# When transfers are issued around a decoder's last cross attention: gated weights, kept tokens, and the first two weight blocks of the MLP

## The chip, the cores and the metric

The kernel runs on one core of a Trainium2 chip. The time is device microseconds (us) of one execution. The kernel before takes 1160.57 us, the median of three runs (1159.35 to 1161.3). Engines are named as in the profile: PE is TensorE, DVE is VectorE, ACT is ScalarE, POOL is GpSimd, SP is SyncE, which here issues almost all DMAs.

## The reference

Sixteen sequences x of 128 tokens and 512 features go through a decoder layer and then through a gated cross attention. Both attend to sequences of the same shape, ctx_2048. All is float32, with 16 heads of 32 features. In short:

```python
# decoder layer
ln = layernorm(x);   q, k, v = split(ln @ w_qkv + b_qkv)
x = x + merge(attention(q, k, v, ltor_mask)) @ w_ao + b_ao          # sections A0..A3
ln = layernorm(x);   q = ln @ w_q + b_q
k, v = split(ctx_2048 @ w_kv + b_kv)
x = x + merge(attention(q, k, v, cross_mask)) @ w_co + b_co         # sections B0..B3
ln = layernorm(x);   x = x + gelu(ln @ w1 + b1) @ w2 + b2           # w1: 512x2048, w2: 2048x512
# gated cross attention
a = layernorm(ctx_2048)
Q, K, V = x @ Wq.T, a @ Wk.T, a @ Wv.T
x = x + tanh(gate) * (merge(softmax(mask(Q K^T * scale)) V) @ Wo.T) # sections D0..D3
```

## The kernel before, in words

**Sections and steps.** The sixteen sequences are cut into four groups of four. The decoder's attention runs as eight sections, self attention A0 to A3 and then cross attention B0 to B3, one for each group. A section has 16 steps (`attend`, line 685): a step works on one unit, that is four of the sixteen heads of one sequence. In the first of a sequence's four steps PE makes the scores of all heads. The units then go down a chain, one step behind the other: DVE scales the scores, POOL adds the mask, DVE takes the least, ACT takes the exponential, POOL divides by the sums, and DVE transposes 32x32 squares (`turn_unit`, line 598). SP sends the result to DRAM (`away_B<-s_B`, 256 KB a unit). Some steps later it fetches two units at a time, in four transfers of 128 KB (`receive_pair`, line 621, `pT_B<-away_B`), so that the probabilities lie turned. PE mixes the values with them (`av_B`) and two steps later makes the output product (`mo_B`). The pT tiles have three buffers. In the last section, steps go on past 15 until all is mixed.

**Beside a section** other work is placed by hand, by step: `jobs()` of section n+1 (its projections) and `prepare(p)` of section n+2 run in section n's steps. `plan(...)` takes pairs of a list of jobs and a list of their steps. What stands behind B3 is `first`, a `FirstGated`: its `prepare` runs beside B2, and `beside_last_cross()` (line 1721) gives the jobs beside B3: the first gated section's keys and values (`mm_k_D`, `mm_v_D`, whose weights are `w_gk` and `w_gv`), the beginning of the MLP, and the return of x3.

**x3, put away and back.** Each cross section's group of tokens x[g] lends three of its four blocks as room for sums (`tokens_at` in `CrossAttention.jobs`). These blocks are first put away in DRAM (`kept_x_B`) and come back by `tokens_again(steps, order)` (line 1065), before the output products add to them. For B0 to B2 they come back in steps 5, 9 and 13 of the next section, for B3 in steps 1, 1 and 3 of its own.

**Gated weights.** Turned once, early in the kernel, and kept in DRAM as `kept_gk` and `kept_gv`. `FirstGated.prepare` loads each in four pieces of 256 KB, one a step: gk in steps 8 to 11 beside B2, gv in steps 12 to 15. All large weights share a pool of six buffers (tag "w").

**The MLP** (`mlp`, a generator) has 16 rounds n, four groups by four blocks i of 512 hidden features. A round has seven places r, and in each a product of the hidden layer (`h`) and one of the output of the round before (`o`). Products are by quarters with seven products in place of eight, so each weight block needs four sums of its quarters (`weight_sums`, tile t, 1 MB). For the first group these sums are made and put away in DRAM for the other three: `kept<-t`. For round 0 that is done at fixed places, (0, 3) and (1, 3). For later rounds it is a fifth entry of the list `todo` that `sums` returns (line 1222). In round n the sums of w2's block n and of w1's block n+1 stand in one queue, `todo`, and two entries are done at each r. Round 0 begins in step 17 of B3.

`w1_0` is loaded in four pieces beside B2 (steps 12 to 15). Then `pieces` holds four pieces each of `w2_0` and `w1_1`, and `loads` gives the steps beside B3 in which they are issued. `w2_1` and `w1_2`, 1 MB each, are loaded whole in round 0 at r = 1 and r = 2.

**What sets the order.** Every instruction is kept in program order on its engine (`InOrder`). SP takes its DMAs strictly one after the other: one that waits for data holds all behind it. Each also waits until the transfer issued eight places before it has landed. `due()` runs what was put off with `afterwards("act" or "dve", ...)`, at the next step or the next place of the MLP.

Of the kernel before, what the change touches and what calls it, by code (L numbers as in the profile page):

```python
# [10 lines left out]
F32 = mybir.dt.float32  # L11
# [5 lines left out]
P = 128  # L17
# [4 lines left out]
H = 512  # L22
NH = 16
HD = 32
KC = H // P
HALF = H // 2
GB = 4
# [27 lines left out]
def decoder_then_gated_cross_attention(ctx: ExitStack, tc: tile.TileContext, a: dict, out: bass.AP):  # L55
    nc = InOrder(tc)

    cpool = ctx.enter_context(tc.tile_pool(name="const", bufs=1))
    wpool = ctx.enter_context(tc.tile_pool(name="weights", bufs=6))
# [98 lines left out]
    w = {}  # L158
# [843 lines left out]
    class CrossAttention(Section):  # L1002
# [34 lines left out]
        def jobs(self):  # L1037
            g, n, lnT, encT = self.g, self.name, self.lnT, self.encT
            mask = work.tile([P, 2, GB, S], F32, tag="mask", name=f"mask_{g}", bufs=2)
            self.ms, self.ma = mask[:, 0], mask[:, 1]  # L1040
            nc.sync.dma_start(
                out=self.ms, in_=a["mask_Bx1xSxS2_ff1"][g * GB : (g + 1) * GB, 0].rearrange("b q k -> q b k")
            )
            qkv_tiles(self)
            tokens_at = [x[g][:, b].rearrange("p (o t) -> p o t", t=HF) for b in range(3)]
            token_sides, sums = right_blocks(encT, tokens_at)
            if g == 0:
                self.begin()
            products = [
                block_product(halves(self.k), self.k_sides, token_sides, False, f"k_{n}", ("b_k", 0)),  # L1050
                block_product(by_quarters(self.v), self.v_sides, token_sides, True, f"v_{n}"),
            ]
            return plan(
                ([lambda c=c: self.query_chunk(c) for c in range(KC)], [0, 1, 3, 5]),
                *blocks_plan(products, CROSS_BLOCKS if g else FIRST_CROSS_BLOCKS), ([lambda: mask_terms(self.ms, self.ma)], [7]),
                ([lambda o=o: nc.gpsimd.tensor_tensor(*o) for o in sums], [0, 1, 2, 3]),
                *(self.weights_begin() if g == 0 else decoder[NG + g - 1].tokens_again([5, 9, 13])),
            )

        def query_chunk(self, c):  # L1060
# [117 lines left out]
    def mlp(ml, last_steps):  # L1178
# [17 lines left out]
        def load(n, which):  # L1196
            g, i = steps[n]
            ap, r0, c0 = (a["L0_xattn_w1"], 0, i * H) if which == 1 else (a["L0_xattn_w2"], i * H, 0)
            wt = wpool.tile([P, KC, H], F32, tag="w", name=f"w{which}_{n}")
            src = ap[r0 : r0 + H, c0 : c0 + H].rearrange("(k p) n -> p k n", p=P)  # L1200
            if n < 2 and not (n == 1 and which == 2):
                for k in range(KC):
                    pieces.append(lambda k=k: nc.sync.dma_start(out=wt[:, k], in_=src[:, k]))
            elif g == 0:
                nc.sync.dma_start(out=wt, in_=src)
            else:
                nc.sync.dma_start(out=wt[:, 0:2, 0:HF], in_=src[:, 0:2, 0:HF])
                nc.sync.dma_start(out=wt[:, 2:4, :], in_=src[:, 2:4, :])
            return wt
# [114 lines left out]

        w1[0] = load(0, 1)
        yield
        w2[0], w1[1] = load(0, 2), load(1, 1)
        right1[0], todo, _ = sums(0, 1, "enc", w1.pop(0), nc.gpsimd)
        yield
        for do in todo:  # L1330
# [7 lines left out]
        for n in range(len(steps) + 1):  # L1338
            todo, more = deque(), []
            at_ = {r: [] for r in range(7)}  # L1340
            h = lnT = None
            if n + 1 < len(steps):
                right1[n + 1], more, back = sums(n + 1, 1, "v", w1.pop(n + 1))
                at_[3].append(back)
            if n < len(steps):
                g, i = steps[n]
                right2[n], first, back = sums(n, 2, "enc", w2.pop(n))
                todo.extend(first + more)
                at_[4].append(back)
                h = work.tile([P, KC, TG], F32, tag="qT", name=f"h_{n}", bufs=2)  # L1350
                if i == 0 and n:
                    sides = following
                if g + 1 < NG and i == 1:
                    at_[0].append(lambda: ml_begin(g + 1))
                    for b in range(GB):
                        at_[b].append(lambda b=b: ml_send(g + 1, b))
                elif g + 1 < NG and i == 2:
                    lnT = turned_tile(g + 1)
                    at_[0].append(lambda: ml_receive(g + 1))
                    for m in range(NQ):  # L1360
                        at_[m // 2].append(lambda m=m: ml.part(m))
                    for c in range(KC):
                        at_[3 + c].append(
                            lambda c=c: chunk_back(lnT[c // 2][:, c % 2], ml.back, c, "ln3_s", "ln3_b")
                        )
                    next_lnT = lnT
                elif g + 1 < NG and i == 3:
                    following, more = sums_of(g + 1, next_lnT)
                    for r, do in enumerate(more):
                        at_[3 + r].append(do)  # L1370
            if before is not None:
                for r, do in enumerate(before[1]):
                    at_[r].append(do)
            for r in range(7):
                if n < len(steps):
                    p = H_ORDER[r]
                    hidden_product(n, p, sides[p], right1[n][p], h)
                if before is not None:
                    p = O_ORDER[r]
                    out_product(n - 1, p, before[0][p], right2[n - 1][p], acc)  # L1380
                for _ in range(min(2, len(todo))):
                    todo.popleft()()
                for do in at_[r]:
                    if do is not None:
                        do()
                if r == 1 and n + 1 < len(steps):
                    w2[n + 1] = load(n + 1, 2)
                elif r == 2 and n + 2 < len(steps):
                    w1[n + 2] = load(n + 2, 1)
                last_steps(n, r)  # L1390
                if (n, r) in ((0, 3), (1, 3)):
                    d, t = unkept.pop(0)
                    nc.sync.dma_start(out=d, in_=t)
                yield
            if n < len(steps):
                t = work.tile([P, 3, 2, HF], F32, tag="kT", name=f"sh_{n}", bufs=2)
                before = token_sums(halves(h), t[:, 0], t[:, 1], t[:, 2])


    gated = {}  # L1400
# [56 lines left out]

    class FirstGated:


        def prepare(self, p):
            if p == 0:
                self.raw = work.tile([P, GB, H], F32, tag="enc", name="enc_D0", bufs=2)
                self.ln, self.away = ln_tile("D0"), away_tile("D0")
            if p in (0, 1):
                for b in (2 * p, 2 * p + 1):
                    nc.sync.dma_start(out=self.raw[:, b, :], in_=a["ctx_2048"][b])
            elif p >= 2 * GB:
                key, k = ("gk", "gv")[p // GB - 2], p % GB
                if k == 0:  # L1470
                    w[key] = wpool.tile([P, KC, H], F32, tag="w", name=f"w_{key}")
                nc.sync.dma_start(out=w[key][:, k], in_=gated[key][:, k])
            if 2 <= p < 6:
                q = p - 2
                normalize_and_send(self.raw[:, q, :], self.ln[:, q], self.away, "D0", q)
            if p >= 12:
                if p == 12:
                    next(in_mlp)
                ml.pieces.popleft()()
            if p in (9, 11):  # L1480
                if p == 9:
                    self.back, self.part = receiver("a0", self.away)
                for m in range(2):
                    self.part(m + 2 * (p == 11))
            if p >= 12:
                if p == 12:
                    self.aT = act_tile("a0", "enc")
                group_back(self.aT, self.back, "gamma", "beta", [p - 12])
# [228 lines left out]
    ml = Mlp()  # L1717
# [3 lines left out]
    def beside_last_cross():  # L1721
        flip[0], in_blocks[0] = 2, False
        def piece():
            due()
            next(in_mlp)

        at_ = [2, 3, 4, 5, 6, 15, 15, 16, 16, 17, 18, 19, 19, 20, 21, 21, 22, 23, 23]
        loads = [5, 7, 9, 11, 13, 14, 15, 16]
        return plan(
            *gated_start(first), *mlp_start(ml), *decoder[-1].tokens_again([1, 1, 3], (1, 0, 2)), ([piece] * len(at_), at_),  # L1730
            ([lambda: ml.pieces.popleft()()] * len(loads), loads),
        )

# [94 lines left out]
```

## Time and profile before

| what | us |
| --- | --- |
| median of three runs | 1160.57 |
| the profiled execution, as timed | 1162.35 |
| its span in the profile | 1160.6 |
| PE busy in the span | 1132.9 |
| B2, scores at steps 0, 4, 8, 12 | 403.8, 419.9, 434.9, 451.3 |
| B3, scores at steps 0, 4, 8, 12 | 467.2, 483.2, 496.0, 511.9 |
| first product of the MLP's round 0 (step 17) | 526.5 |

Everything in the profile has the source line L51, since a helper records all operations; so one goes by the names of tiles, and by times. A line of the timeline gives start, duration, engine, what is written and read, and in square brackets how long the engine was idle before it and what released it. In the timeline of SP the durations are those of issuing, not of the transfer. In the chain that ended last, a line "DMA a<-b" gives the time from the issue to the landing.

### The profile page before, as it was taken

Reading aid. Unit: us, or ns where it says so; the run is one execution under the profiler, and the core shown is the slowest. Engines: PE = TensorE matmul, PEld = TensorE weight load, DVE = VectorE, ACT = ScalarE, POOL = GpSimd, SP = SyncE. Lnnn points to the kernel's source line nnn. Section 1 sums busy time; section 2 is a strip of 40 time slices with the busy share of each in tenths; the row PEclk is TensorE's granted clock in tenths of the full one; section 3 lists DMA queues with packets and bytes.
Section 4 is the critical chain, followed back from the end, with each engine's and each line's share of the span. In section 5 each row is a group of like instructions: output and inputs, shape, how many; then the busy total and the mean of one; then the engine's idle time right before and its main releaser. Section 6 shows DMA issues by size and latency. Waiting matters only on the chain.

```text
span 1160.6 us, 22182 instructions
## 1 busy us (share of the span) xinstructions
PE 1132.9 (98%) x7246; PEld 875.1 (75%) x7246; DVE 742.9 (64%) x1919; ACT 612.0 (53%) x2142; POOL 694.4 (60%) x633
## 2 busy tenths in 40 slices
PE   9999999999999999989899999999999999999998
PEld 8877777666666757446688888888888877878875
DVE  6678978798787786866554634443342247767754
ACT  3567676767767766663231233223222237867663
POOL 6798888788868675752333514443342168545883
PEclk9999999999999999989999999999999999999999
DMA  6688878999889889997787696697447827987975
GB/s 220 162 206 227 228 208 212 280 232 255 209 221 222 218 231 254 297 272 247 236 260 238 189 280 192 200 283 254 154 154 234 258 51 200 249 236 222 272 216 175
DMA packets 325285, 259.81 MB, mean 224 GB/s; under 512 B 83561, under 2 KB 280625, under 8 KB 320305
## 3 DMA queue, kind: packets, MB, share of 16 engines
q1 hardware_dynamic: 325128, 258.38, 78.1%
q8 instruction: 58, 0.95, 0.4%
q14 instruction: 59, 0.48, 0.1%
q10 hardware_dynamic: 40, 0.01, 0.0%
HBM read 163.94 MB, written 94.37 MB: 223 GB/s over the span
## 4 chain that ended last, share of the span: by engine, by line
PE 45%; DMA 6%; POOL 2%; DVE 2%; SPq 1%; ACT 1%; issue 1%; DVEq 0%; ACTq 0%; POOLq 0%
PE o L51 16%; PE h L51 15%; PE mm_v_D L51 4%; PE mm_q_D L51 3%; PE mm_o_D L51 1%; DMA back_x<-turned_x 1%; DMA pT_D<-away_D 1%; PE mm_k_D L51 1%; DMA pT_B<-away_B 1%; SPq L51 1%; PE av_D L51 1%; DMA away_D<-s_D 1%; PE mo_D L51 1%; DMA away_B<-s_B 1%; PE sc_D L51 1%
## 5 line engine op out<-in xcount | busy, mean ns | idle before, releaser
L51 DVE TENSOR_TENSOR h<-h,h 128x512 f32<-128x512 f32 x80 | 54.9, 686 | 113.9 <-PE h L51 113.9
L51 ACT ACTIVATE h<-h 128x512 f32<-128x512 f32 x64 | 40.3, 630 | 162.3 <-DVE h L51 162.3
L51 ACT ACTIVATE s_A<-s_A,mn_A 128x128 f32<-128x128 f32 x256 | 99.4, 391 | 45.7 <-issue 23.8
L51 ACT ACTIVATE s_B<-s_B,mn_B 128x128 f32<-128x128 f32 x256 | 99.4, 392 | 29.7 <-issue 14.0
L51 POOL TENSOR_TENSOR s_D<-s_D,sum_D 128x512 f32<-128x512 f32 x64 | 66.5, 1040 | 59.9 <-DVE sum_D L51 53.1
L51 POOL TENSOR_TENSOR s_B<-s_B,sum_B 128x512 f32<-128x512 f32 x64 | 66.8, 1044 | 56.4 <-DVE sum_B L51 47.8
L51 ACT ACTIVATE s_D<-s_D,mn_D 128x128 f32<-128x128 f32 x256 | 99.1, 392 | 0.4 <-issue 0.4
L51 POOL TENSOR_TENSOR s_A<-s_A,sum_A 128x512 f32<-128x512 f32 x64 | 66.5, 1039 | 31.0 <-DVE sum_A L51 25.3
L51 POOL TENSOR_TENSOR s_A<-s_A,ma 128x512 f32<-128x512 f32 x64 | 81.8, 1279 | 5.1 <-DVE s_A L51 4.1
L51 POOL TENSOR_TENSOR s_B<-s_B,mask 128x512 f32<-128x512 f32 x60 | 76.4, 1273 | 2.4 <-DVE s_B L51 1.5
L51 POOL TENSOR_TENSOR rstd_aD<-rstd_aD,mhalf 128x1 f32<-128x1 f32 x12 | 6.6, 549 | 114.8 <-DVE rstd_aD L51 101.6
L51 POOL TENSOR_TENSOR sh<-h 128x512 f32<-128x512 f32 x32 | 40.7, 1272 | 50.8 <-ACT h L51 49.9
L51 PE MATMUL h<-sx,t 128*128 128x256 f32 x256 | 60.6, 379 | 2.0 <-ACT h L51 2.0
L51 PE MATMUL h<-T_C,w 128*128 128x256 f32 x256 | 61.2, 382 | 1.3 <-DVE h L51 1.3
L51 PE MATMUL h<-T_C,t 128*128 128x256 f32 x256 | 60.6, 379 | 1.0 <-DVE h L51 1.0
L51 PE MATMUL o<-t,h 128*128 128x256 f32 x256 | 60.5, 379 | 0.0
L51 PE MATMUL o<-w,h 128*128 128x256 f32 x256 | 60.5, 379 | 0.0
L51 PE MATMUL o<-t,sh 128*128 128x256 f32 x256 | 60.5, 379 | 0.0
L51 DVE CUSTOM_DVE_ANT_0 s_D<-sc_D,gmask 128x128 f32<-128x128 f32 x256 | 57.1, 283 | 1.0 <-DMA turned_x<-x_D 0.9
L51 PE MATMUL mo_A<-w_ao,mT_A 128*128 128x512 f32 x128 | 57.5, 592 | 0.0
L51 PE MATMUL mo_B<-w_co,mT_B 128*128 128x512 f32 x128 | 57.5, 592 | 0.0
L51 PE MATMUL mm_q_B<-T_B,w_cq 128*128 128x512 f32 x128 | 57.4, 596 | 0.0
(335 smaller groups left out, 3007.4 us busy)
## 6 DMA issues: line engine op xcount, KB each, us to landing
t<-kept SPq DMA_DIRECT2D x24, 1024.0 KB, 8.3
away_A<-s_A SPq DMA_DIRECT2D x64, 256.0 KB, 3.3
pT_A<-away_A SPq DMA_DIRECT2D x128, 128.0 KB, 3.8
away_B<-s_B SPq DMA_DIRECT2D x64, 256.0 KB, 3.3
pT_B<-away_B SPq DMA_DIRECT2D x128, 128.0 KB, 4.8
away_D<-s_D SPq DMA_DIRECT2D x60, 256.0 KB, 3.4
pT_D<-away_D SPq DMA_DIRECT2D x120, 128.0 KB, 2.8
w<-in_L_xattn_w_dram SPq DMA_DIRECT2D x24, 512.0 KB, 5.5
```

Of the source, the lines that this page charges most:

```text
L51: return lambda *args, **kw: self.tc.keep_in_program_order(call(*args, **kw))
```

## The change

No operation is added or taken away; on PE, ACT and POOL the instructions and their order are the same. Four places are edited. gk is loaded in steps 14, 14, 15, 15 beside B1, as jobs of B2, and gv in steps 6 to 9 beside B2. x3's blocks come back in steps 6, 10 and 14 of B3, in the order 0, 1, 2. `w1_1` stands ahead of `w2_0` in `pieces`, and the eight pieces are issued in steps 7 to 17. In round 0 alone, `todo` holds w1's entries ahead of w2's. The line numbers of the diff are those of the two files.

```diff
@@ -1055,6 +1055,10 @@  CrossAttention.jobs
                 *(self.weights_begin() if g == 0 else decoder[NG + g - 1].tokens_again([5, 9, 13])),
+                *(
+                    [([lambda k=k: first.fetch_weight_part("gk", k) for k in range(KC)], [14, 14, 15, 15])]
+                    if g == 2 else []
+                ),
             )
@@ -1324,7 +1328,7 @@  mlp
         w1[0] = load(0, 1)
         yield
-        w2[0], w1[1] = load(0, 2), load(1, 1)
+        w1[1], w2[0] = load(1, 1), load(0, 2)
         right1[0], todo, _ = sums(0, 1, "enc", w1.pop(0), nc.gpsimd)
@@ -1345,7 +1349,7 @@  mlp, in round n
                 right2[n], first, back = sums(n, 2, "enc", w2.pop(n))
-                todo.extend(first + more)
+                todo.extend(first + more if n else more + first)
@@ -1457,6 +1461,11 @@
     class FirstGated:
+        def fetch_weight_part(self, key, k):
+            if k == 0:
+                w[key] = wpool.tile([P, KC, H], F32, tag="w", name=f"w_{key}")
+            nc.sync.dma_start(out=w[key][:, k], in_=gated[key][:, k])
+
@@ -1465,11 +1474,8 @@  FirstGated.prepare
-            elif p >= 2 * GB:
-                key, k = ("gk", "gv")[p // GB - 2], p % GB
-                if k == 0:
-                    w[key] = wpool.tile([P, KC, H], F32, tag="w", name=f"w_{key}")
-                nc.sync.dma_start(out=w[key][:, k], in_=gated[key][:, k])
+            elif 6 <= p < 10:
+                self.fetch_weight_part("gv", p - 6)
@@ -1725,9 +1731,9 @@  beside_last_cross
-        loads = [5, 7, 9, 11, 13, 14, 15, 16]
+        loads = [7, 9, 11, 13, 14, 15, 16, 17]
         return plan(
-            *gated_start(first), *mlp_start(ml), *decoder[-1].tokens_again([1, 1, 3], (1, 0, 2)), ([piece] * len(at_), at_),
+            *gated_start(first), *mlp_start(ml), *decoder[-1].tokens_again([6, 10, 14]), ([piece] * len(at_), at_),
```

In the built order of SP's DMAs the last transfers beside B3 change as follows; on DVE the eight sums of `w2_0` and `w1_1` change places.

```
before: w2_1, away_B, w1_2, kept<-t (w1_0), pT_B x4, kept<-t (w1_1)
after:  w2_1, away_B, w1_2, kept<-t (w1_1), kept<-t (w1_0), pT_B x4
```

## The prediction

> **What bounds the kernel now.** I read the busy shares first, then who TensorE (PE) waited for, then PE's timeline at the waits, the DMA share of the same stretches, SyncE's (SP's) issues, and the chain that ended last. The page says that PE is the bound:
>
> ```profile
> PE 1132.9 (98%) x7246; PEld 875.1 (75%) x7246; DVE 742.9 (64%) x1919; ACT 612.0 (53%) x2142; POOL 694.4 (60%) x633
> ```
>
> So the change can only win what PE idles, or add to it: 1160.6 less 1132.9 is 27.7 us in all. PE's waits between 440 and 575 us, where all edits act, name it:
>
> ```profile
> PE av_B L51 <- DMA pT_B<-away_B: 6.7, 2, 5.5
> PE h L51 <- ACT h L51: 2.0, 1, 2.0
> ```
>
> PE's timeline shows where these stand. Square brackets are idle time:
>
> ```profile
> 466.18 1.07 PE L51 MATMUL av_B<-pT_B,v_B 128*32 128x128 f32 x28 [1.12 <-DMA pT_B<-away_B]
> ...
> 510.09 1.92 PE L51 MATMUL av_B<-pT_B,v_B 128*32 128x128 f32 x28 [5.54 <-DMA pT_B<-away_B]
> ...
> 551.57 1.63 PE L51 MATMUL av_B<-pT_B,v_B 128*32 128x128 f32 x32
> 555.16 1.99 PE L51 MATMUL h<-sx,t 128*128 128x256 f32 x8 [1.96 <-ACT h L51]
> ```
>
> I call them stall 1 (466, step 0 of the last cross section, B3), stall 2 (510, B3 step 12) and the tail (552, step 22). At each, probabilities that went out to DRAM come back (pT) too late for a mix (av). The tail's mix is almost late too: its 32 matmuls take 1.63 us against 1.08 us elsewhere. Stall 2 costs more than its 5.54 us, for the clock is halved after it, and the same is seen after a gap of only 2.31 us at 1027 (columns: us, then PE, PEld, DVE, ACT, POOL busy, granted clock, DMA share, GB/s):
>
> ```profile
> 510.00:516.00 6.00, 5.91 (x63) 4.30 (x64) 1.92 (x10) 3.89 (x14) 0.11 (x1) 0.50 1.08 301
> ...
> 1024.60:1028.00 3.40, 1.09 (x32) 0.83 (x28) 3.40 (x15) 0.45 (x3) 2.73 (x3) 1.00 1.02 288
> 1028.00:1031.40 3.40, 3.40 (x11) 2.73 (x9) 0.17 (x2) 0.58 (x1) 2.65 (x3) 0.50 1.09 282
> ```
>
> The same view by stage shows the transfers. A share about 1 means that all 16 DMA engines are busy; then what SP issues waits behind what it issued before:
>
> ```profile
> 446.00:482.00 36.00, 34.88 (x226) 21.96 (x224) 28.97 (x64) 23.02 (x84) 21.25 (x21) 1.00 1.07 294
> 482.00:490.00 8.00, 8.00 (x78) 4.37 (x78) 7.03 (x14) 6.57 (x28) 8.00 (x8) 1.00 0.91 265
> 490.00:512.00 22.00, 16.46 (x128) 8.49 (x126) 14.49 (x29) 12.52 (x58) 17.63 (x16) 0.94 1.08 272
> ```
>
> **Part 1: gk and gv sooner.** Eight 256 KB pieces move, none is added. gk goes from steps 8 to 11 of B2 (436.5 to 447.6) to steps 14 and 15 of B1, where SP issues nothing between 395.7 and 399.3, and the DMA share from 396 to 408 is 0.41: 1 MB at 0.3 MB/us is 3.5 us of room that exists; PE waits for no DMA there. Cost 0. gv goes from steps 12 to 15 of B2 to steps 6 to 9 (428.7 to 438, share 0.69): cost 0. Its first piece gains a wait for PE; the buffer should be that of the query weight, the one that falls free there. The last query product (`mm_q_B`, 423.51, 3.6 us) ends at 427.1; SP gets there at 428.7, behind a `turned_D` send that waits for DVE. If that cover went, the next probabilities' send would be held as long. Two gk and two gv pieces thus vanish from SP's order between 446 and 459.4, ahead of the pT that ends stall 1: 1 MB, at 294 GB/s 3.6 us. The stall is 1.12. **Gain 1.1 us**, and nothing else is late next in that place.
>
> **Part 2: x3 back later.** Three 256 KB pieces leave 469.7, 470.7 and 479.1 for steps 6, 10 and 14 of B3. Their first reader, the addition of `mo_B` after step 14 (DVE at 524.6), comes over 20 us after the step-6 piece, and the third piece's reader is at 543.7. Cost 0 there. Do they relieve stall 2? Only if the queue of 446 to 482 carries over. At 479.7 SP waits 2.4 us for DVE (its next probabilities turned), which it could not if the DMAs were behind, and the share falls to 0.91. So the group that makes stall 2 starts at 482, and in it the change takes out one piece (w2 at step 5) and puts in one (x3 at step 6). Steps 7 and 9 hold w1 instead of w2, same size; the other x3 piece, step 10, is issued behind the late pT. **Stall 2: 0.** Bounds: a piece more or less, 256 KB at 272 GB/s, 0.95 us either way.
>
> **Part 3: w1's second block ahead of w2's first.** The pieces of both are eight before and after, at steps 7 to 17 in place of 5 to 16. DVE's eight sums are the same instructions in another order (0.67 to 1.41 us each); w2's last piece, issued about 532, should land near 536, and DVE reads it at about 536.5: 0, bound +1. But the swapped `todo` also moves an instruction that is not a sum. The list of w1's second block ends with its put-away, a 1 MB transfer to DRAM (`kept<-t`, line 1222). It was the ninth entry, so it stood behind the last pT. It becomes the fifth, and in the built order of SP it stands, with w1's first put-away, **ahead of the last pT**. SP now:
>
> ```profile
> 538.78 0.51 SPq L51 DMA_DIRECT2D w<-in_L_xattn_w_dram  x1
> 539.33 1.08 SPq L51 DMA_DIRECT2D kept<-t  x1
> 544.47 2.13 SPq L51 DMA_DIRECT2D pT_B<-away_B  x4
> 546.70 0.43 SPq L51 DMA_DIRECT2D kept<-t  x1
> ```
>
> What that costs is read from the chain, and from the DVE instruction that waited for the first `kept<-t`:
>
> ```profile
> 538.30 6.09 DMA away_B<-s_B
> ...
> 545.94 6.05 DMA pT_B<-away_B
> ```
>
> ```profile
> 549.64 0.69 DVE L51 TENSOR_TENSOR t<-w 128x512 f32<-128x512 f32 x1 [1.78 <-DMA kept<-t]
> ```
>
> The probabilities' send landed at 544.39, the put-away issued after it at 549.62, with one 1 MB load between: 5.2 us for two such transfers, 2.6 us each. The pT, issued at 544.5 to 546.6, landed at 552.00, behind the put-away. One more put-away in front makes that 554.6. Everything behind is serial: av, ACT's copy of the mix, ACT's h, PE's h at 555.16. DVE's wait for the first put-away grows by as much, and in parallel. **Loss 2.6 us**; bounds 0 (if the pT passes the put-away) and 2.6.
>
> Then the clock. PE's idle time at the tail becomes 0.55 + 2.6 = 3.1 us, followed by 1.08 of work and 1.96 idle. The row at 1024.6 halved the clock for 3.4 us after 2.31 idle, so I expect it here. 3.4 us at half is 1.7 lost, less what falls on the 1.96 us in which PE waits anyway: **loss 1.0**, bounds 0 and 1.7.
>
> [...] The row at 1024.6 gated after 2.31, so I keep the loss. [...] Here the landings kept their order.
>
> **Sum.** −1.1 + 0 + 2.6 + 1.0 = +2.5 us. The profiled execution took 1162.35 us (span 1160.6), 1.8 more than the median of the three runs, 1160.57 (1159.35 to 1161.3). The difference is put on the median: **1163.1 us**.
>
> **The rivals.** What a measurement can tell from no change is about 0.2%, 2.3 us: 1158.2 to 1162.9.
>
> - *Faster: the queue carries over to stall 2.* The share between 482 and 490 is still 0.91, not 0.5. If transfers from before 482 still hold those after it, nine pieces fewer (two gk, four gv, three x3; 2.25 MB, 8 us) bring the pT of step 10 in early. Stall 2 goes with its clock (three groups, 1.92 against 1.08, 2.09 against 1.17, 4.71 against 3.70: 2.8): −1.1 − 5.5 − 2.8 + 3.6 = −5.8, 1154.8. It decides as soon as that pT lands some 3 us earlier, since a short gap spares the clock: 1163.1 − 3 − 2.8 = 1157.3. Against it is SP's wait for DVE at 479.7.
> - *Same: the tail is paid but the clock is not halved, or lightly:* −1.1 + 2.6 = +1.5, 1162.1. [...] Or the last pT is not held: 1159.5.
> - *More slower: stall 2 grows.* The x3 piece at step 6 goes into the group that is late, beside four reads of `turned_C`. A read of kept x took a median 6.2 us to land between 446 and 482, where gv took 4.7. That is 1 us (one piece) to 3 us (two slow reads): 1164.1 to 1166.1.
>
> **How the numbers follow.** Tail with clock, 1163.1: 0.46, of which 0.06 fall under the line at 1162.9. Stall 2 grows: 0.10. Tail without clock: 0.16. Last pT not held: 0.06. Faster, 1154.8 to 1157.3: 0.22. Slower by over 0.2% is 0.40 + 0.10 = 0.50; within, 0.06 + 0.16 + 0.06 = 0.28; faster 0.22. The range takes in half of the faster case, from 1156.5, and most of a grown stall 2 with the full clock loss (+0.7) and w2's late piece (+1), to 1167: about 0.17 is left out. The likeliest case alone is 1162.1 to 1164.8.
>
> **What would show it.** Part 1: no DMA wait of PE near 466, DMA share of 446 to 466 under 1. Part 2: PE's wait near 509 still 5 to 6.5 us, clock 0.50 after it; a wait under 3 us means that the queue carried over, and that I am wrong on the side of faster. Part 3: SP issues two `kept<-t` before the last four pT; PE's wait at the tail's av about 3 us, released by that pT; a granted clock of 0.50 near 556. A wait of DVE for w there means that w2's last piece is late.

## The result, and the profile after

The changed kernel takes 1163.21 us, median of 10 runs (1160.87 to 1166.13). The kernel before, in 10 runs beside it, takes 1159.3 (1157.8 to 1161.3). The ratio is 1.0036, 95% interval 1.0024 to 1.0047: slower by 2.8 to 5.4 us. The profiled execution of the changed kernel took 1166.13 us, with a span of 1164.3, 3.7 more than the span before.

PE is busy for 1.0 us more than before, so the rest of what was lost in this profile is idle time. This line is from the first part of the page:

```profile
PE 1133.9 (97%) x7246; PEld 876.1 (75%) x7246; DVE 742.8 (64%) x1919; ACT 611.9 (53%) x2142; POOL 694.6 (60%) x633
```

PE's waits between 440 and 576 us (total, times, longest) name the same transfer as before, with 9.1 us in place of 6.7:

```profile
PE av_B L51 <- DMA pT_B<-away_B: 9.1, 4, 6.9
PE h L51 <- ACT h L51: 2.0, 1, 2.0
```

PE's timeline of the changed kernel shows where. There is no wait near 466 any more; the other two have grown:

```profile
510.69 1.92 PE L51 MATMUL av_B<-pT_B,v_B 128*32 128x128 f32 x28 [6.95 <-DMA pT_B<-away_B]
...
554.04 1.07 PE L51 MATMUL av_B<-pT_B,v_B 128*32 128x128 f32 x28 [1.74 <-DMA pT_B<-away_B]
557.07 3.78 PE L51 MATMUL h<-sx,t 128*128 128x256 f32 x8 [1.96 <-ACT h L51]
560.64 3.15 PE L51 MATMUL o<-w,h 128*128 128x256 f32 x8
```

The last two lines are at half clock: 3.78 and 3.15 us in place of 1.99 and 1.89. DMA shares by stage in the changed kernel (the last two columns) show less traffic before the group that makes stall 2, and as much in it:

```profile
446.00:482.00 36.00, 36.00 (x257) 22.81 (x257) 28.72 (x64) 22.86 (x84) 21.16 (x22) 1.00 0.87 241
482.00:490.00 8.00, 8.00 (x60) 4.09 (x51) 7.01 (x14) 6.43 (x27) 8.00 (x8) 1.00 0.73 203
490.00:512.00 22.00, 14.78 (x120) 7.64 (x120) 14.64 (x29) 12.66 (x60) 17.79 (x16) 0.92 1.07 284
```

And SP's timeline, between the last send and the last pT, has two put-aways where there was one. The chain that ended last has that pT with 8.47 us from issue to landing in place of 6.05:

```profile
538.71 1.63 SPq L51 DMA_DIRECT2D kept<-t  x2
543.89 2.15 SPq L51 DMA_DIRECT2D pT_B<-away_B  x4
```

```profile
545.43 8.47 DMA pT_B<-away_B
```

The same instructions in the two traces, by their start, give the account. Its first two rows are these lines, before and then after:

```profile
426.95 3.60 PE L51 MATMUL mo_B<-w_co,mT_B 128*128 128x512 f32 x8
467.18 1.17 PE L51 MATMUL sc_B<-k_B,q_B 32*128 32x128 f32 x32
```

```profile
427.45 3.60 PE L51 MATMUL mo_B<-w_co,mT_B 128*128 128x512 f32 x8
466.17 1.17 PE L51 MATMUL sc_B<-k_B,q_B 32*128 32x128 f32 x32
```

"Lead" is after less before; the step is what the stretch above the line added:

| PE instruction | before | after | lead | step |
| --- | --- | --- | --- | --- |
| `mo_B`, 427 (the lead is the same at 351, ahead of all edits) | 426.95 | 427.45 | +0.50 | |
| scores after stall 1 | 467.18 | 466.17 | −1.01 | −1.5 |
| mix after stall 2 | 510.09 | 510.69 | +0.60 | +1.6 |
| `mo_B`, behind the halved clock | 518.51 | 518.50 | 0.0 | −0.6 |
| `h` after the tail's mix | 555.16 | 557.07 | +1.91 | +1.9 |
| `h<-T_C,w`, two products on | 559.38 | 563.63 | +4.25 | +2.3 |
| `h<-T_C,t` | 570.97 | 575.11 | +4.14 | −0.1 |

So stall 1 was won and handed back 40 us later. All that is left at the end was lost at the tail: 1.9 us of waiting, and 2.3 us of half clock behind it. The loss at the tail stands in other profiles too: from the `mo_B` near 518 to `h<-T_C,t` it is 52.46 us before, 56.61 in the changed kernel, and 56.76 in a second profile of it (e5 below). The spans of single profiles are no measure of the change, though: behind `h<-T_C,t`, where no edit acts, the 14 profiles take from 585.4 to 591.7 us, and the span of e5, 1159.6, is below that of before.

### The profile page after: what moved, and what is told of

Read it like the earlier page. It is cut to its first block, busy times and chain, and to the rows that moved or that the text cites. A ratio compares the mean times of both kernels' runs of the same rounds, so it can differ in the third digit from the quotient of the medians.

```text
span 1164.3 us, 22177 instructions
## 1 busy us (share of the span) xinstructions
PE 1133.9 (97%) x7246; PEld 876.1 (75%) x7246; DVE 742.8 (64%) x1919; ACT 611.9 (53%) x2142; POOL 694.6 (60%) x633
## 4 chain that ended last, share of the span: by engine, by line
PE 47%; DMA 4%; POOL 3%; DVE 3%; issue 2%; SPq 1%; ACT 1%; POOLq 0%; DVEq 0%; ACTq 0%
PE o L51 16%; PE h L51 16%; PE mm_v_D L51 4%; PE mm_q_D L51 3%; PE mm_k_D L51 2%; DMA pT_B<-away_B 2%; PE av_D L51 1%; PE mo_B L51 1%; PE sc_D L51 1%; PE mm_o_D L51 1%; POOL s_D L51 1%; DVE s_D L51 1%; SPq L51 1%; POOL x L51 1%; PE mo_D L51 1%
```

## Experiments

The theory after this reading, called A: the loss is the put-away of w1's second block ahead of the last pT, and the clock that its wait brings down; the gain of part 1 is given back at stall 2. Rivals: the tail's wait matters little and stall 2, grown by x3's piece, costs the time (D); or the clock at the tail falls anyway. Each kernel was timed beside the kernel before on the same chip (median of before there: 1160.67 for e1 to e4, 1161.47 for e5 to e8, 1160.74 for e9 to e12). Waits are PE's, in us, in the one profile that each kernel has.

| kernel | ratio to before, 95% | stall 2 | tail's mix | us at half clock after stall 2 / the tail |
| --- | --- | --- | --- | --- |
| before | 1 | 5.54 | 0 | 6.8 / 0 |
| changed | 1.0036, 1.0024 to 1.0047 | 6.95 | 1.74 | 6.8 / 6.8 |
| e1, put-away last | 0.9995, 0.9977 to 1.0014 | 6.82 | 0.42 | 6.8 / 3.4 |
| e2, before with one more put-away | 1.0042, 1.0024 to 1.0061 | 4.44 | 2.52 | 6.8 / 6.8 |
| e3, parts 1 and 2 | 1.0020, 1.0000 to 1.0039 | 6.76 | 1.08 | 10.2 / 3.4 |
| e4, 64 small matmuls at the tail | 1.0040, 1.0023 to 1.0057 | 7.85 | 0 | 6.8 / 0 |
| e5, changed again | 1.0028, 1.0011 to 1.0045 | 6.27 | 2.08 | 6.8 / 6.8 |
| e6, 32 small matmuls | 0.9999, 0.9987 to 1.0011 | 6.53 | 0.59 | 6.8 / 3.4 |
| e7, light group | 1.0006, 0.9991 to 1.0021 | 3.41 | 3.20 | 0 / 6.8 |
| e8, e1 and value products sooner | 0.9987, 0.9971 to 1.0003 | 2.90 | 1.41 | 0 / 3.4 |
| e9, e8 and light group | 0.9977, 0.9958 to 0.9995 | 0.18 | 0 | 0 / 3.4 |
| e10, e9 and 16 small matmuls | 0.9973, 0.9957 to 0.9989 | 0 | 0 | 0 / 0 |
| e11, x3 out of the group | 1.0021, 1.0004 to 1.0039 | 5.06 | 2.05 | 6.8 / 6.8 |
| e12, part 1 alone | 0.9991, 0.9975 to 1.0007 | 5.18 | 0.21 | 6.8 / 3.4 |

### The put-away: e1 takes it away, e2 adds it

e1 is the changed kernel with the put-away behind the sums of w2:

```diff
-                todo.extend(first + more if n else more + first)
+                todo.extend(first + more if n else more[:-1] + first + more[-1:])
```

> The changed kernel, with the 1 MB put-away of w1's second block moved back behind the last four pT transfers; w1's sums still stand ahead of w2's. Theory A (the tail's loss is that put-away ahead of the last pT, and the clock that the longer gap halves): PE's wait at the tail's av falls from 1.74 us to under 0.5, the granted clock stays at 1.00 near 556, and the time falls by 1.6 + 2.3 = 3.9 us, from 1163.2 to about 1159.3; parts 1 and 2 of the change are worth nothing, since stall 2 takes back what stall 1 gives. Rival B (the loss is stall 2 grown by 1.4 us and the order of the sums on DVE): the time stays above 1161.5.

e2 is the kernel before with a second put-away of w1's first block, 1 MB to a spare place in DRAM, issued behind the first one and so ahead of the last pT:

```diff
+                    if n == 0:
+                        spare = dram.tile([P, 4, 2, HF], F32, tag="spare", name="spare")
+                        nc.sync.dma_start(out=spare, in_=t)
```

> The kernel before, with one transfer added and nothing else: w1's first block of sums is put away twice (the second time to spare room), so that one more 1 MB transfer stands ahead of the last four pT. Theory A: the last pT lands about 2.6 us later, PE's wait at the tail's av is 2 to 3 us, and the granted clock is halved near 556; the time rises by 2.6 + 1.0 to 2.6 + 2.3, from 1159.3 to between 1162.5 and 1164.2. Rival B (a transfer there is hidden): 1159.3 to 1160.3.

e1 took 1160.8 us, 0.9995, and e2 1165.64, 1.0042. SP's timeline and PE's in e1:

```profile
538.69 1.41 SPq L51 DMA_DIRECT2D kept<-t  x1
546.42 1.79 SPq L51 DMA_DIRECT2D pT_B<-away_B  x4
548.25 0.43 SPq L51 DMA_DIRECT2D kept<-t  x1
```

```profile
552.89 1.07 PE L51 MATMUL av_B<-pT_B,v_B 128*32 128x128 f32 x28 [0.42 <-DMA pT_B<-away_B]
555.92 3.35 PE L51 MATMUL h<-sx,t 128*128 128x256 f32 x8 [1.96 <-ACT h L51]
```

With one put-away ahead of it, the last pT ends a wait of 0.42 us and not of 1.74, and the time is that of before. This one line of `todo` makes the difference between a kernel that is slower and one that is not told apart from before. e2 shows the other direction: in the kernel before, which has none of the other edits, one more put-away alone makes a wait of 2.52 us where there was none, halves the clock for 6.8 us, and costs as much as the change. A part of e1's expectation failed: the clock does not stay at 1.00, it is halved for 3.4 us (8 matmuls in 3.35 us): PE is busy for 1.45 of the 3.41 us ahead of it.

### The parts: e3, e12, e11, and the changed kernel again

e3 is the changed kernel without part 3 (load order, load steps and `todo` of before). e12 is e3 without part 2 as well, that is part 1 alone. e11 is the changed kernel with x3's pieces out of stall 2's group. e5 is the changed kernel, unaltered, for comparison on the same chip as e6 to e8.

```diff
 e3, e12:
-        w1[1], w2[0] = load(1, 1), load(0, 2)
+        w2[0], w1[1] = load(0, 2), load(1, 1)
-                todo.extend(first + more if n else more + first)
+                todo.extend(first + more)
-        loads = [7, 9, 11, 13, 14, 15, 16, 17]
+        loads = [5, 7, 9, 11, 13, 14, 15, 16]
 e12 also:
-            ... decoder[-1].tokens_again([6, 10, 14]) ...
+            ... decoder[-1].tokens_again([1, 1, 3], (1, 0, 2)) ...
 e11, from the changed kernel:
-            ... decoder[-1].tokens_again([6, 10, 14]) ...
+            ... decoder[-1].tokens_again([11, 12, 14]) ...
```

> The changed kernel without part 3: gk, gv and x3 move as in the change, but w2's first block is loaded ahead of w1's second in the steps of before, and the sums and put-aways have the order of before. In B3 up to step 10 this has one more 256 KB piece than before. Theory A (what stall 1 gives back, stall 2 takes, because the pT of step 10 does not land sooner when PE comes sooner): no wait at 466, PE's wait at stall 2 6.5 us or more, time 1159.3, within 1 us. Rival C (part 1 is worth its 1.1 us): 1158.2 or less. Rival D (the x3 piece in the group of transfers before stall 2 costs net time): 1160.5 or more.

> The kernel before with part 1 alone: gk and gv sooner, x3 back where it was, w2's first block ahead of w1's second, put-away last. Theory A (the gain of stall 1 is given back at stall 2, since the pT there is issued by what VectorE and GpSimd turn and lands at the same time however early PE comes): no wait of PE near 466, stall 2 at 6.4 to 6.8 instead of 5.54, ratio 0.999 to 1.001. Theory D (stall 2 grew because of x3's piece in its group): with x3 out of the group stall 2 stays at 5.5 or below and the 1.1 us of stall 1 remain a gain, ratio 0.998 to 0.999.

> The changed kernel with x3's pieces at steps 11, 12 and 14 of B3 instead of 6, 10 and 14; w1's pieces stay. Theory A (every 256 KB in the group costs the same 0.95 us): one piece fewer ahead of the late pT, which lands 0.9 us sooner, stall 2 near 6.0, clock still halved behind it: 0 to 1 us faster than the changed kernel, ratio 1.002 to 1.003. Theory D (the read of kept x is slow beside the four reads of turned_C and costs 1 to 3 us): stall 2 at 4 to 6, 1 to 3 us faster, ratio 1.000 to 1.002.

> The changed kernel once more and unaltered, so that the three below have it on their own chip. Expected: 1.0036 of the kernel before, within its interval 1.0024 to 1.0047.

Measured: e3 1162.28 (1.0020), e12 1159.9 (0.9991), e11 1163.52 (1.0021), e5 1164.73 (1.0028). In time these intervals overlap, and e11 is not told apart from the changed kernel. Nor is e3 quite what theory A wants: it has the put-away last as e1 has, and is yet at 1.0020; the two intervals meet only between 1.0000 and 1.0014. Why is not settled; in its one profile e3 has 10.2 us at half clock behind stall 2, and e1 6.8. The waits say more. The mix at stall 2, in the profile of e12 and of e11:

```profile
509.46 1.92 PE L51 MATMUL av_B<-pT_B,v_B 128*32 128x128 f32 x28 [5.18 <-DMA pT_B<-away_B]
```

```profile
508.52 1.92 PE L51 MATMUL av_B<-pT_B,v_B 128*32 128x128 f32 x28 [5.06 <-DMA pT_B<-away_B]
```

Sorted by whether x3's piece of step 6 is in the group, the waits do not mix. With it, and with no other edit to the group but w2's piece, stall 2 is 6.95, 6.82, 6.76, 7.85, 6.27 and 6.53 (changed, e1, e3, e4, e5, e6). Without it it is 5.54, 4.44, 5.18 and 5.06 (before, e2, e12, e11). That looks like rival D. But a wait grows for two reasons: the pT lands later, or PE comes to it sooner, and in before and e2 PE comes later, since they still have stall 1. PE's timeline tells the two apart, since the mix begins as the pT lands (in the changed kernel 0.14 us behind it at the tail, at 554.04 and 553.90). Counted in us from the start of `mo_B` near 427:

| kernel | x3's piece | scores after stall 1 | mix after stall 2 |
| --- | --- | --- | --- |
| before | no | 40.23 | 83.14 |
| e2 | no | 39.73 | 81.41 |
| e12 | no | 38.48 | 82.39 |
| e11 | no | 38.47 | 80.77 |
| changed | yes | 38.72 | 83.24 |
| e1 | yes | 38.67 | 82.73 |
| e3 | yes | 38.66 | 83.40 |
| e4 | yes | 38.47 | 83.95 |
| e5 | yes | 38.47 | 81.98 |
| e6 | yes | 38.56 | 82.32 |
| e7, e9 (last section of the experiments) | no, nor w1's | 38.47 | 79.12, 79.32 |

By these times the first ten do mix: 80.8 to 83.1 without x3's piece, 82.0 to 84.0 with it, and kernels that are alike up to there differ by as much (before and e2 by 1.7; changed, e1, e4, e5 and e6 by 2.0). From before to the changed kernel PE comes 1.51 sooner, and the mix begins only 0.10 later. So nearly all the growth of this wait is PE's coming sooner to a pT that comes when it did; the change takes one piece out of the group (w2 at step 5) and puts one in (x3 at step 6). Rival D's mechanism, x3's piece making the pT late, is not shown: e11 has one piece fewer than the changed kernel and the earliest mix of the ten, 80.77, but that is one profile. That pieces in the group hold this pT is shown by e7 and e9, which take three out (two of w1, one of x3): their mix begins 2.7 us before the earliest of the kernels with x3's piece.

Theory A's part "the gain of stall 1 is given back because the pT lands at the same time however early PE comes" fits this, though its number for e12 was not met: it expected 6.4 to 6.8 us at stall 2, and there were 5.18. A wait of 1.10 us at 494.70, which before does not have, took most of the difference: 1.10 and 5.18 are 6.28, where before waits 1.12 at stall 1 and 5.54, 6.66:

```profile
494.70 1.07 PE L51 MATMUL av_B<-pT_B,v_B 128*32 128x128 f32 x28 [1.10 <-DMA pT_B<-away_B]
```

So most of stall 1's gain is given back in that profile too, part of it one mix sooner than was thought. In time e12 is 0.9991; neither a gain of 1 us nor none is excluded.

### The clock: e4 and e6

Both are the changed kernel with small matmuls in the last mix, ahead of the late pT, on the pair of probabilities that is already there; the real mix writes over their output. e4 has 4 times 16, e6 2 times 16; the edit shown is e6's.

```diff
+        for c in [c for _ in range(2) for c in range(KC)] if bt.name == "B3_3" else ():
+            for j in (0, 1):
+                h = c * GB + j
+                nc.tensor.matmul(
+                    av[j * HD : (j + 1) * HD, c * S : (c + 1) * S], sec.v[:, b, h * HD : (h + 1) * HD],
+                    bt.pT[j][:, :, c, :], start=True, stop=True,
+                )
```

> The changed kernel, with 64 matmuls of the last mix, on the pair of pT that is there, done four times over ahead of it (they are written again by the mix itself), so that PE works in place of idling while it waits for the last pT. Nothing else moves. Theory A (the halved clock near 556 comes of the idle gap, and costs 2.3 us): the last pT lands as late as before, the clock stays at 1.00 there, and the time falls from 1163.2 to about 1160.9. Rival B (the halved clock has another cause, or what it takes is hidden behind waits): 1162.7 to 1163.7.

> The changed kernel with the busy work ahead of the last mix cut to two rounds of 16 matmuls (at the 0.87 us a round that the run with four showed, 1.75 us, which is what PE waits there; four rounds took 3.5 us and outlasted the wait). Theory A (the halved clock behind the tail comes of the idle gap and costs 2.3 us): the clock stays at 1.00 behind it and the time is 1.5 to 2.5 us under that of the changed kernel on the same chip. Rival B (it costs nothing, since PE waits there anyway): within 0.7 us of the changed kernel.

e4 took 1165.46 (1.0040). It kept the clock at 1.00 but was sized badly: 16 of these matmuls take 0.87 us, so 64 outlast the wait. PE's timeline in e4, where the 96 are the 32 of the mix and the 64 added:

```profile
553.12 4.56 PE L51 MATMUL av_B<-pT_B,v_B 128*32 128x128 f32 x96
559.68 1.99 PE L51 MATMUL h<-sx,t 128*128 128x256 f32 x8 [2.00 <-ACT h L51]
```

`h` runs at 1.99 us again, but starts at 559.68 and not at 557.07: the clock's price was paid in matmuls. e6, with 1.75 us of them, fits. It took 1161.92, 0.9999, 2.8 us under the changed kernel on the same chip (1164.73, e5). The pT is no earlier in it (the mix is at 554.01, against 554.04 in the changed kernel's profile), so what it wins is not waiting. The half clock there is one stretch of 3.4 us in place of 6.8, and `h<-T_C,t` starts at 573.76 in place of 575.11:

```profile
573.76 1.99 PE L51 MATMUL h<-T_C,t 128*128 128x256 f32 x8 [0.98 <-DVE h L51]
```

So 1.3 us of the loss are seen to be the clock in this pair of profiles, and can be had without the pT coming sooner. The time says 2.8. The other 1.5 are not found in the two profiles at this place, but the granted clock of all twelve executions of each kernel has room for them: its mean is 0.9936 in e5 and 0.9966 in e6. Of 1161 us that is 7.0 us less at half clock, two stretches of 3.4 and not one, or 3.5 us of lost clock.

### What a faster kernel needs: e7, e8, e9, e10

e7 is the changed kernel with w1's and x3's pieces put behind the pT of stall 2. e8 is e1 with the third and fourth gated value product two steps sooner, to fill stall 2 with work. e9 is e8 with e7's steps, e10 is e9 with 16 of the small matmuls.

```diff
 e7, e9, e10:
-        loads = [7, 9, 11, 13, 14, 15, 16, 17]
+        loads = [11, 12, 13, 13, 14, 15, 16, 17]
-            ... decoder[-1].tokens_again([6, 10, 14]) ...
+            ... decoder[-1].tokens_again([11, 12, 14]) ...
 e8, e9, e10 (with e1's line):
-            ([lambda b=b: value_job(b) for b in range(GB)], [7, 9, 13, 15]),
+            ([lambda b=b: value_job(b) for b in range(GB)], [7, 9, 11, 13]),
```

> The changed kernel with the four 256 KB pieces that it issues in steps 6, 7, 9 and 10 of B3 (x3, w1, w1, x3) issued in steps 11 to 13 instead; three of them stood ahead of the late pT of step 10. Theory Q (stall 2 is set by the queue of transfers issued from 482 us on, some 25 pieces of 256 KB at 0.95 us): that pT lands about 2.8 us sooner, PE's wait at stall 2 falls from 6.95 to about 4 us, and the time falls by 2.5 to 3 us against the changed kernel, more if the clock is spared. Theory P (stall 2 is set by when DVE and POOL have the probabilities ready, not by the queue): the wait stays over 6 us and the time within 1 us.

> The run with the put-away last, and besides the third and fourth block of the gated values (mm_v_D, 3.6 us of PE each) in steps 11 and 13 of B3 in place of 13 and 15. Step 11 is that in which PE has nothing and waits for the pT of step 10. Theory A (PE's wait at stall 2 is for a transfer that does not mind when PE comes): the wait falls by 3.5 us to about 3.3 us, and the time by 3.5 us against the run with the put-away last, to about 0.997 of the kernel before; with a spared clock 0.995. Rival: the value block's own transfer to DRAM comes sooner too and delays the pTs behind it, and the time falls by less than 1.5 us.

> Put-away last again, gated value products one step pair sooner, and the light group (w1's pieces and x3's behind the late pT) together. Theory A (the pT that ends stall 2 waits only for the transfers issued in its own group): that pT lands near 507 instead of 510.6, the value product that now stands ahead of the mix takes 3.7 us, so PE waits there under 1 us and the clock stays 1.00 from 490 to 540; the waits at 530 and at the tail keep 1 to 3 us in all, because the pieces are now issued between the steps there. Ratio to the kernel before 0.997 to 0.998. Theory B (the DMA engines have the same bytes to move from 482 to 560, so every wait removed comes back at the next pT): the waits at 530 and 552 grow by what stall 2 loses; ratio 0.9987 as without the light group, or above.

> As the kernel before it in this list, and 16 small matmuls of the pair of probabilities that is already there (0.87 us of PE, their output is written over by the real mix) in the last mix ahead of the late pT. Theory A (the clock is halved at the tail by idle time inside one window, and keeping PE busy there spares it): the granted clock stays 1.00 or its half part gets shorter, 0.5 to 1.5 us faster than without them, ratio 0.996 to 0.997. Theory B (the 1.96 us in which PE waits for ScalarE's h are enough by themselves to halve the clock): no difference, or 0.5 us slower where the pT had landed already.

e7: 1162.25, 1.0006, 2.5 us under the changed kernel on the same chip (the two intervals overlap a little). SP issues the pT of stall 2 at 500.84 in place of 502.56, it lands at 507.04 in place of 510.56, the wait is halved and the clock stays (1.00 from 490 to 536):

```profile
507.17 1.07 PE L51 MATMUL av_B<-pT_B,v_B 128*32 128x128 f32 x28 [3.41 <-DMA pT_B<-away_B]
```

The pieces come back later, though: waits of 2.26 us at 530.54 and 3.20 at the tail. e8: 1160.57, 0.9987; e9: 1157.94, 0.9977; e10: 1158.03, 0.9973. The last two are faster than the kernel before, by about 2.7 and 3.1 us. PE's timeline of e9 has stall 2 at almost nothing, but what was taken from it stands again at 529.68:

```profile
506.00 1.07 PE L51 MATMUL av_B<-pT_B,v_B 128*32 128x128 f32 x28 [0.18 <-DMA pT_B<-away_B]
...
529.68 1.92 PE L51 MATMUL av_B<-pT_B,v_B 128*32 128x128 f32 x28 [3.90 <-DMA pT_B<-away_B]
```

PE's waits for pT between 440 and 576 sum to 5.7 us in e8, 5.0 in e9, 4.7 in e10. So e9's theory B is right in its mechanism, most of the wait came back at the next pT, and its number (0.9987 or above) was not met only by a difference that the intervals of e8 and e9 don't separate. Its clock is halved for 3.4 us behind the wait at 529.68, which e9's theory A did not expect. e10's clock stays at 1.00 at the tail, as its theory A had it (and is halved for 3.4 us behind the wait at 531); the time against e9 is the same within the intervals, so its 0.5 to 1.5 us are not shown.

## Why the prediction came out as it did

The predicted time was 1163.1 and the median is 1163.21; but the median of before also moved, from 1160.57 in three runs to 1159.3 in ten. The change itself is +3.9 us (2.8 to 5.4) where the sum said +2.5. By its steps, in the order of the sum:

- **Stall 1, −1.1: right at that place, but not kept.** The account gives −1.5 in that stretch, of which 1.12 is the wait that is gone. DMA share 0.87 in place of 1.07.
- **Stall 2, 0: wrong, and outside its bounds of 0.95.** The wait is 6.95 in place of 5.54, and the account's step is +1.6. The count behind the zero, one piece out and one in, is borne out: counted from `mo_B` at 427 the mix begins at 83.14 before and at 83.24 after. The step that failed is "Gain 1.1 us, and nothing else is late next in that place", added to the sum as a gain that lasts. The next late thing was the pT of stall 2: PE came to it 1.51 us sooner, it came when it did, and PE waited that much longer. The third rival had the size (1 to 3 us); its mechanism, the slow read of x3, is not shown. A little came back: the halved clock behind the later mix falls on less work (−0.6; of 6.83 us at half clock, 5.94 lie behind the start of the mix before, and 4.70 after). It was right that the queue of 446 to 482 does not carry over: the share of 482 to 490 fell to 0.73, and the pT came no sooner.
- **Tail, +2.6: right in mechanism, 1.9 in the account.** Two put-aways land 2.64 us apart (548.97 and 551.61), as worked out, and the last pT behind them at 553.90. But SP reached this group 0.6 us earlier than before (its send of probabilities at 537.66, before 538.30), so it landed 1.9 later and not 2.6. e1 and e2 show the cause from both sides.
- **Clock at the tail, +1.0: mis-sized, 2.3 measured, beyond the bound of 1.7.** The sum took one stretch of 3.4 us from the row at 1024.6. It was 6.83 us, from 556.35 on (last section). Its other error was to think that this needs a gap of 2 or 3 us: the waits there are 1.74 and 1.96 us.
- **w2's last piece, 0:** no wait of DVE or PE for it appears; right.

So −1.1 became −0.5 by the end of stall 2, and +3.6 became +4.2. The direction and the place were right; the two terms of the tail erred in opposite directions, and the term called zero was not zero. That 1163.1 lies 0.1 from the median is luck: the time it started from was 1.3 above that of the ten runs, and the sum was 1.4 short.

On the clock the prediction was not of one mind: its first rival says that a short gap spares it, where its own row had 2.31 us and a halved clock. No run shows such a rule: at the tail of the changed kernel no wait was longer than 1.96 us and the clock was halved for 6.83 us, while e7's wait of 3.41 us left it at 1.00. On the last pT, the order of landing held: the landings that the two traces give for what SP issued between 537 and 547 us come in the order of issue, 543.68, 544.39, 549.62, 552.00 and 554.57 before, and 543.08, 548.97, 551.61 and 553.90 in the changed kernel.

## What to carry to other kernels

When entries of a work list are reordered, follow every instruction that an entry issues down to its queue: here the sums were harmless, and a 1 MB store that rode along in the list decided the result. A wait that is taken away is a gain only if the next one does not take it back: ask when the next late transfer lands, counted from a place ahead of the edits, and do not go by the length of its wait alone. And a short wait ahead of a dependent chain is priced with its clock, as here, where waits of 1.74 and 1.96 us brought 2.3 us of half clock with them: look at what else PE idles in the same few microseconds.

## What the runs showed of the hardware

**The granted clock around the waits.** In the changed kernel's trace the granted clock is 0.50 from 508.56, 556.35 and 1030.80 us on, for 6.83, 6.83 and 3.41 us; in that of before from 509.21 and 1028.03 on, for 6.83 and 3.41 us. Between 30 and 1150 us it is 1.00 elsewhere in both. The length of a wait alone does not tell whether the clock is halved: e7's wait of 3.41 us left it at 1.00, and PE's wait of 1.96 us for `h` at the tail has no half clock behind it in the kernel before, 3.4 us in e1 and 6.83 in the changed kernel. The stretches below are 3.41 us long, counted from a change of the clock in the same trace. The tail of the changed kernel (length, then PE busy first, granted clock third from last):

```profile
552.94:556.35 3.41, 1.07 (x28) 0.83 (x28) 1.26 (x5) 1.21 (x5) 1.78 (x2) 1.00 0.60 65
556.35:559.76 3.41, 2.69 (x6) 2.19 (x7) 2.02 (x4) 1.36 (x3) 0.00 (x0) 0.50 0.09 27
559.76:563.18 3.42, 3.42 (x9) 2.70 (x8) 3.11 (x7) 0.81 (x1) 1.78 (x2) 0.50 0.91 280
563.18:566.59 3.41, 3.41 (x17) 3.01 (x16) 2.25 (x6) 0.25 (x1) 1.78 (x2) 1.00 0.20 77
```

Ahead of the halving PE is busy for 1.07 of 3.41 us. Two stretches at half follow, the first with 2.69 us of work, the second full, and behind them the clock is 1.00. The kernel before has this stretch at the tail:

```profile
553.58:557.00 3.42, 1.84 (x9) 1.64 (x10) 1.16 (x2) 2.22 (x7) 0.35 (x1) 1.00 0.47 70
```

PE idles for the same 1.96 us ahead of `h`, but is busy for 1.84 of 3.42, and there is no halving. In e7 the wait of 3.41 us lies across two stretches with 1.61 and 1.81 us of work, and the clock stays at 1.00:

```profile
502.15:505.57 3.42, 1.61 (x7) 0.34 (x6) 3.37 (x7) 2.86 (x14) 3.23 (x4) 1.00 1.10 271
505.57:508.98 3.41, 1.81 (x56) 1.64 (x60) 2.36 (x6) 2.54 (x14) 3.00 (x3) 1.00 1.13 289
```

These are readings of single profiles, in which PE's busy time is modelled; what sets the clock was not shown. The changed kernel's profile has 3.4 us at half clock from 1030.8 on; in that of e5, the same kernel, the mean granted clock of 0.994 leaves no room for as much beside the 6.8 and 6.8 us of the table. The spread of the times goes with the clock: of the 104 executions of the kernel before beside the experiments, the 28 with a mean granted clock of 0.997 or more have a median of 1158.9 us, the 29 with 0.994 or less 1163.6. No run held the clock fixed, so that this makes the spread is likely and not shown.
